# A decoder layer whose projections are FP32 matmuls in 32-column slices in place of three passes over rounded halves

## The chip, the cores and the metric

The kernel runs on one core of one Trainium2 chip (trn2). The metric is the device time of one execution in microseconds, given as the median of the runs. The profile is that of one execution.

## The reference

One pre-norm decoder layer over x of shape 2 x 2048 x 512 and a context of 2 x 154 x 512, all in FP32:

```python
x = x + linear_attention(layernorm(x))          # 16 heads of 32, 128 random features
x = x + cross_attention(layernorm(x), context)  # 16 heads of 32, softmax over 154 keys
x = x + experts(layernorm(x))                   # top 6 of 8 by a softmax router, and a shared one
```

The linear attention projects to q, k and v with `w_qkv` (512 x 1536), takes `elu(q @ proj) + 1` and the same of k as features, sums `k_features^T v` over all keys of a batch, applies it to the queries' features, divides by the sum of features, and multiplies by `w_out`. The cross attention has `x @ W.T + b` for q, k, v and its output, each 512 x 512. The experts are gated units, `silu(h @ gate) * (h @ up) @ down`.

## The kernel before, in words

The 4096 tokens are 8 blocks of 512, four blocks to a batch; a block is four tiles of 128 tokens, and the model dimension of 512 is four chunks of 128. A product of projections is one PSUM bank of 128 x 512, with four chunks to sum over.

Every operand of a product is held as two FP32r tiles (`fp32r` in the profile), the rounded value and what the rounding left. `low` (L116) makes the second: it subtracts the first from the FP32 source. `product` (L144) then makes three matmuls for each chunk, high by high, low by high, high by low, and leaves out low by low. `project` (L151) and `times` (L164) call it for the keys (pk), values (pv), queries (pq) and the cross queries (xpq); `out_tile` (L287) calls it for the two output projections (po_a, po_x), `context_key` and `context_value` for the context's keys (xpk) and values (xpv). The weights are split by `split_weight` (L126), which loads a chunk through the ring of token tiles unless it is loaded already; the layernormed tokens by `transposed` (L240) into the pair xh, xl; the attention by `attended` (at), the cross attention's result by `values` (cx), the context by `context_load`. The experts call `product` too, or have their own loops over the same three terms (L1028, L1141).

The matmuls of linear attention and cross attention that serve single heads are FP32 with 32 columns, into one of four 32-row slices of a bank: the sums over keys (pkv, L397), numerators (pn, L471), denominators (pd, L489) and the context of a head (pc, L720). The scores and features (pp, pqp, psc) use stacked high and low rows of 32 + 32 + 32.

The order of the work is written out by hand as one stream. `Dense` (L175) holds a queue of generators, each a product with its `yield` after every matmul. The stage loops take the features or scores of one step, which the other engines hold up, and before or between them call `dense.fill(n)`, which puts the next n matmuls of the queue; `dense.until` fills until a named tile exists. `dense.after(n, do)` issues a transfer n matmuls later. The stages are:

- L1242: the keys and values of all blocks, with the queries of the first batch from the middle on. Each step is one tile of four key heads: fill, features, and the sums over keys three steps later. Keys and queries go to DRAM and come back stacked by heads (`to_heads`, `stack`, `read`).
- L1285: the second batch's queries; between them the first output projection.
- L1325: cross attention; between its scores the second output projection, the next block's layernorm and the next block's cross queries.
- L1421: the experts.

A scheduler then moves instructions within each engine's stream by a model of their times. All loads of projections' operands go through the queue of SyncE (SP).

Of the kernel before, what the change touches and what calls it, by code (L numbers as in the profile page):

```python
# [19 lines left out]
NC = D // P  # chunks of the model dimension  # L20
# [3 lines left out]
TB = 512  # tokens in a block  # L24
NT = TB // P  # token tiles in a block
# [7 lines left out]
SC = 4  # banks for what is read as soon as it is made  # L33
GROUP = 2  # blocks that a load of an expert serves
# [3 lines left out]
def decoder_layer(  # L38
    ctx: ExitStack,
    tc: tile.TileContext,  # L40
    x: bass.AP,  # [tokens, D]
    ctx_t: bass.AP,  # [D, batch * keys]
    w_qkv: bass.AP,  # [D, 3D]
    proj: bass.AP,  # [HD, H * FEAT]
    w_out: bass.AP,
    b_out: bass.AP,  # [1, D]
    wq_t: bass.AP,  # [in, out], as the three below
# [3 lines left out]
    bq: bass.AP,  # [P, NC]  # L51
    bk: bass.AP,  # [P, NC]
    bv: bass.AP,  # [1, D]
    bo: bass.AP,  # [1, D]
# [13 lines left out]
    bpb = nblk // batches  # blocks of a batch  # L68
# [47 lines left out]
    def low(dst, src, hi, eng=None):  # L116
        """dst = what rounding src to hi left."""
        (eng or nc.vector).tensor_tensor(dst, src, hi.bitcast(F32), ALU.subtract)  # L118

    def load_weight(w, name):  # L120
        raw = eight([P, NC, w.shape[1]], F32, f"raw_{name}")
        for k in range(NC):
            nc.sync.dma_start(out=raw[:, k], in_=w[k * P : (k + 1) * P, :])
        return [raw[:, k] for k in range(NC)]

    def split_weight(raw, name, busy=False):  # L126
        """A weight [D, D] or its loaded chunks as a pair of FP32r parts that sum to it."""
        hi = eight([P, NC, D], FR, f"{name}_hi")
        lo = eight([P, NC, D], FR, f"{name}_lo")
        for k in range(NC):  # L130
            if isinstance(raw, list):
                part = raw[k]
            else:
                part = load_tile(raw, 0, k, name)
            if busy:
                nc.gpsimd.tensor_scalar(hi[:, k], part, 1.0, None, ALU.mult)
            else:
                nc.scalar.copy(hi[:, k], part)
            low(lo[:, k], part, hi[:, k], nc.gpsimd if busy or k % 2 else nc.vector)
        return hi, lo  # L140

    TERMS = ((0, 0), (1, 0), (0, 1))  # all but low times low

    def product(dst, pairs):  # L144
        """dst = sum of a^T b over the pairs (a, b), each of them a (high, low) pair."""
        todo = [(a[i], b[j]) for a, b in pairs for i, j in TERMS]
        for n, (a, b) in enumerate(todo):
            nc.tensor.matmul(dst, lhsT=a, rhs=b, start=n == 0, stop=n == len(todo) - 1)  # L148
            yield

    def project(dst, w, col, src):  # L151
        """dst [P, n] = 128 columns of w, transposed, times src [P, NC, n]."""
        return product(
            dst,
            [
                (
                    (w[0][:, k, col : col + P], w[1][:, k, col : col + P]),
                    (src[0][:, k, :], src[1][:, k, :]),
                )
                for k in range(NC)  # L160
            ],
        )

    def times(dst, src, t, w):  # L164
        """dst [P tokens, n] = the transposed src's tile t, times w."""
        rows = slice(t * P, (t + 1) * P)
        return product(
            dst,
            [
                ((src[0][:, k, rows], src[1][:, k, rows]), (w[0][:, k, :], w[1][:, k, :]))  # L170
                for k in range(w[0].shape[1])
            ],
        )

    class Dense:  # L175
        """Work for the tensor engine that is put, product by product, between the steps of what
        the other engines hold up."""
# [35 lines left out]
        def until(self, made, key):  # L213
            """Fill until made has the key."""
# [8 lines left out]
    def normalize(xs, name, xn=None, pinned=False):  # L223
        """The layernorm of a token tile, in place unless there is an xn."""
# [15 lines left out]
    def transposed(xn, xt, t, name):  # L240
        """A token tile, transposed, into the pair xt of [P, NC, TB]."""
# [25 lines left out]
    def new_xt(name):  # L267
        return [eight([P, NC, TB], FR, f"{n}_{name}") for n in ("xh", "xl")]

# [5 lines left out]
    # A chunk's 4 heads as [high, low, high] of HD rows each, against [high, high, low] on the  # L275
    # other side: one pass over 3 * HD rows is the whole product.
# [10 lines left out]
    def out_tile(name, src, dst, row, parts, w):  # L287
        """dst = src + row + parts (a list over chunks of pairs of [P, tokens]), transposed back,
        times w."""
# [4 lines left out]
        yield from product(po, [(part, (w[0][:, c, :], w[1][:, c, :])) for c, part in enumerate(parts)])  # L294
# [16 lines left out]
    raw = wk  # L311
    wk = [eight([P, NC, D], FR, f"wk_{i}") for i in ("hi", "lo")]
    for t in range(NT):
        pt = ps.tile([P, NC, P], F32, tag="ps", name=f"pt_a0_{t}")
        for c in range(NC):
            nc.tensor.transpose(pt[:, c, :], xs[t][:, c * P : (c + 1) * P], ident)
        hi, lo = (h[:, :, t * P : (t + 1) * P] for h in xts[0])
        a = nc.scalar.copy(hi, pt)
        b = nc.vector.tensor_tensor(lo, pt, hi.bitcast(F32), ALU.subtract)
        c = nc.scalar.copy(wk[0][:, t], raw[t])  # L320
        d = (nc.gpsimd if t % 2 else nc.vector).tensor_tensor(wk[1][:, t], raw[t], wk[0][:, t].bitcast(F32), ALU.subtract)
# [3 lines left out]
    wv = split_weight(wv, "wv")  # L325
# [4 lines left out]
    wq = split_weight(load_weight(w_qkv[:, :D], "wq"), "wq")  # L330
# [10 lines left out]
    def features(src, name, e=None):  # L341
        """src + 1 where src > 0, else exp(src)."""
# [6 lines left out]
    def key_chunk(b, c):  # L349
# [9 lines left out]
        dense.after(8, read)  # L359
# [103 lines left out]
    def numerators(b, c):  # L463
# [36 lines left out]
    def reciprocals(b, pd):  # L500
        """1 / (the denominators of all heads + Z_EPS), spread over the rows of a head."""
# [16 lines left out]
        dense.after(10, turned)  # L518
        dense.after(18 if b < nblk - 1 else 24, stored)
# [16 lines left out]
    def attended(b, c):  # L536
        """The chunk of the block's attention, as a pair."""
        if c == 0:
            ats[b] = [eight([P, NC, TB], FR, f"at{b}_{i}") for i in range(2)]
        at = nums[b][:, c]  # L540
        nc.gpsimd.tensor_tensor(at, at, zrs.pop((b, c)), ALU.mult)
        nc.scalar.copy(ats[b][0][:, c], at)
        low(ats[b][1][:, c], at, ats[b][0][:, c])

    def attention_out(b, t):
# [3 lines left out]
        hi, lo = ats[b]  # L549
        parts = [(hi[:, c, rows], lo[:, c, rows]) for c in range(NC)]  # L550
        yield from out_tile(f"a{b}_{t}", tile_of(x, b, t), tile_of(x1[b], 0, t), bout, parts, wout)

# [20 lines left out]
    def context_load():  # L573
        craw = eight([P, NC, nkeys], F32, "craw")
        nc.sync.dma_start(out=craw, in_=chunked(ctx_t))
        for i in range(2):
            ct.append(eight([P, NC, nkeys], FR, f"ct{i}"))
        nc.scalar.copy(ct[0], craw)
        low(ct[1], craw, ct[0], nc.gpsimd)

    def context_key(c, w):
        pk = bank(f"xpk{c}")[:, :nkeys]
        yield from project(pk, w, c * P, ct)
# [7 lines left out]
    def context_value(bt, first, w, row):  # L591
# [3 lines left out]
        yield from product(  # L595
            pv[:n, :],
            [
                (
                    (ct[0][:, k, at : at + n], ct[1][:, k, at : at + n]),
                    (w[0][:, k, :], w[1][:, k, :]),  # L600
                )
                for k in range(NC)
            ],
        )
# [29 lines left out]
    qts, xsts, es, atts, cxs = {}, {}, {}, {}, {}  # L634

    def cross_query(b, c):
# [3 lines left out]
        yield from project(pq, xwq, c * P, qts[b])  # L640
# [45 lines left out]
    def turn(b, c, t):  # L686
        """The tile's softmax, transposed."""
# [21 lines left out]
    def values(b, c):  # L709
        """The context of the chunk's 4 heads, transposed."""  # L710
        if c == 0:
            cxs[b] = [eight([P, NC, TB], FR, f"cx{b}_{i}") for i in range(2)]
# [16 lines left out]
        nc.scalar.copy(cxs[b][0][:, c], pc)  # L729
        low(cxs[b][1][:, c], pc, cxs[b][0][:, c])  # L730

    def cross_out(b, t):
        if b < 0:
            return
        hi, lo = cxs[b]
        rows = slice(t * P, (t + 1) * P)
        parts = [(hi[:, c, rows], lo[:, c, rows]) for c in range(NC)]
# [814 lines left out]
```

## Time and profile before

| | |
|---|---|
| runs, median (lowest to highest) | 2378.93 us (2378.63 to 2380.4), 3 runs |
| span of the profiled execution | 2379.7 us |
| instructions in it | 35130 |
| TensorE matmuls in it | 11978, of which pk, pv, pq, po_a, xpq and po_x 384 each |
| first features of queries (pqp) | at 240.5 us |
| first scores of the cross attention (psc) | at 685.5 us |
| first product of the experts (pg) | at 1080.9 us |
| mean granted TensorE clock | 0.990 |

The span runs from the first to the last instruction of the program; the profiled execution's own time is this span, and it lies inside the range of the three runs. A row such as `L148 PE MATMUL xpq<-...` gives line, engine, operation, output and inputs; `128*32 128x512` is rows by columns of the stationary operand and the shape of the moving one. PEld is the loading of stationary operands, which overlaps PE. In a row of the time order the first number is the start, the second the time that it and the merged ones after it cover. In the table of stretches each engine's busy time stands in the order PE, PEld, DVE (VectorE), ACT (ScalarE), POOL (GpSimd), followed by the granted clock, the share of the DMA engines' time and GB/s.

### The profile page before, as it was taken

To read this page: it belongs to the slowest core of one execution; us is meant where nothing else is said; L and a number is where in the kernel's file an instruction comes from. 1 tells how busy PE (TensorE), PEld (TensorE's weight loads), DVE (VectorE), ACT (ScalarE), POOL (GpSimd) and SP (SyncE) were. 2 spreads that over 40 slices of the span, in tenths; PEclk is the share of its full clock that TensorE was granted. 3 is DMA by queue.
4 is the path that set the end of the run, shared out by engine and by line. 5 is a ranking of instruction groups with operands and counts; after the bars stand their busy time and mean duration, and the time that the engine had idled before them with its cause. 6 is when DMAs were issued, how large, how long until landed. Compare 5 with 4: busy or idle time off the path is not lost.

```text
span 2379.7 us, 35130 instructions
## 1 busy us (share of the span) xinstructions
PE 2304.3 (97%) x11978; PEld 1739.1 (73%) x11978; DVE 1673.4 (70%) x2777; ACT 1107.8 (47%) x2598; POOL 1217.5 (51%) x1086
## 2 busy tenths in 40 slices
PE   7999999999999999998999989999999999999999
PEld 5777666655556776775778777888778888778887
DVE  7544554456767776777877787677887778977677
ACT  4555666655546776776433333322333223432221
POOL 5444333364537565554655553554565455754543
PEclk9999999999999999998999999999999999999999
DMA  6555767698876556663766655565547555575653
GB/s 210 175 171 166 195 188 190 189 288 227 232 209 188 169 172 176 173 201 135 274 248 224 230 190 213 203 229 212 219 169 274 203 203 217 208 257 193 228 186 128
DMA packets 194896, 485.63 MB, mean 204 GB/s; under 512 B 26970, under 2 KB 46810, under 8 KB 174782
## 3 DMA queue, kind: packets, MB, share of 16 engines
q1 hardware_dynamic: 192990, 477.30, 60.8%
q0 software_dynamic: 1728, 6.09, 0.9%
q8 instruction: 95, 1.56, 0.3%
q14 instruction: 83, 0.68, 0.1%
HBM read 345.01 MB, written 138.31 MB: 203 GB/s over the span
## 4 chain that ended last, share of the span: by engine, by line
PE 73%; DVE 10%; DMA 7%; POOL 4%; issue 3%; ACT 2%; SPq 1%; DVEq 0%; ACTq 0%; POOLq 0%
PE pg L1028 24%; PE pf L1141 10%; PE pq L148 4%; PE pk L148 4%; PE pv L148 3%; PE po_a L148 3%; PE po_x L148 3%; PE pf L148 3%; PE xpq L148 3%; PE pd L489 2%; PE pkv L397 2%; PE pp L382 2%; PE pc L720 2%; PE pqp L457 2%; PE pn L471 2%
## 5 line engine op out<-in xcount | busy, mean ns | idle before, releaser
L1028 PE MATMUL pg<-xo,wq 128*128 128x512 f32 x3360 | 827.0, 393 | 7.2 <-ACT s L1039 3.4
L1028 PEld LDWEIGHTS pg<-xo,wq 128*128 128x128 f32 x3360 | 630.8, 189 | 149.9 <-ACT s L1039 7.2
L1162 DVE TENSOR_TENSOR sum<-sum,pf 128x512 f32<-128x512 f32 x376 | 250.6, 683 | 61.0 <-PE pf L1141 53.5
L387 POOL TENSOR_TENSOR kacc<-kacc,e_k 128x512 f32<-128x512 f32 x128 | 165.5, 1294 | 242.0 <-DVE e_k L346 220.0
L678 ACT ACTIVATE xe<-psc,nb 128x154 f32<-128x154 f32 x512 | 194.3, 404 | 69.5 <-DVE nb L675 56.2
L683 POOL TENSOR_TENSOR xe<-xe,sm 128x616 f32<-128x616 f32 x128 | 157.3, 1237 | 98.9 <-DVE sm L682 64.3
L1091 POOL TENSOR_TENSOR u<-u,gr 128x512 f32<-128x512 f32 x48 | 63.8, 1329 | 255.4 <-DVE u L1060 245.8
L1141 PE MATMUL pf<-ht,wdo 128*128 128x512 f32 x696 | 187.4, 393 | 1.1 <-DVE sum L1162 1.1
L346 DVE SCALAR_TENSOR_TENSOR e_k<-pp,e_k 128x512 f32<-128x512 f32 x128 | 87.4, 686 | 142.2 <-ACT e_k L345 132.4
L1141 PE MATMUL pf<-hb,wdo 128*128 128x512 f32 x522 | 148.2, 399 | 5.9 <-DVE sum L1162 5.8
L1141 PEld LDWEIGHTS pf<-ht,wdo 128*128 128x128 f32 x696 | 129.8, 188 | 30.7 <-DVE sum L1162 1.7
L1059 ACT ACTIVATE u<-u 128x512 f32<-128x512 f32 x80 | 50.6, 632 | 212.2 <-DVE u L1048 209.4
L148 PE MATMUL pf<-wd,hp 128*128 128x512 f32 x528 | 134.0, 400 | 6.0 <-DVE hp L118 2.7
L675 DVE TENSOR_REDUCE nb<-psc 128x2 f32<-128x308 f32 x256 | 111.7, 466 | 24.3 <-PE psc L668 23.7
L148 PEld LDWEIGHTS pf<-wd,hp 128*128 128x128 f32 x528 | 99.7, 190 | 32.9 <-DVE hp L118 3.7
L1141 PEld LDWEIGHTS pf<-hb,wdo 128*128 128x128 f32 x522 | 97.4, 189 | 30.3 <-DVE sum L1162 7.6
L344 ACT ACTIVATE e_k<-pp 128x512 f32<-128x512 f32 x128 | 76.5, 598 | 88.4 <-PE pp L382 85.4
L1048 DVE TENSOR_TENSOR u<-u,pg 128x512 f32<-128x512 f32 x160 | 107.8, 680 | 10.8 <-PE pg L1028 10.0
L678 ACT ACTIVATION_READ_ACCUMULATOR xe<-psc,nb 128x1 f32 x512 | 112.3, 219 | 0.0
L382 PEld LDWEIGHTS pp<-pst,kst 96*128 96x128 f32 x512 | 75.1, 190 | 29.0 <-issue 12.0
L668 PEld LDWEIGHTS psc<-xkst,xst 96*128 96x128 f32 x512 | 76.6, 193 | 25.3 <-issue 9.2
L668 PE MATMUL psc<-xkst,xst 96*128 96x154 f32 x512 | 90.4, 285 | 4.4 <-ACT xe L678 2.8
(280 smaller groups left out, 5185.7 us busy)
## 6 DMA issues: line engine op xcount, KB each, us to landing
wq<-wqs SPq DMA_DIRECT2D x90, 1024.0 KB
wqs<-wq SPq DMA_DIRECT2D x30, 1024.0 KB
wdo<-wds SPq DMA_DIRECT2D x29, 1024.0 KB
kst<-kd SPq DMA_DIRECT2D x96, 256.0 KB
qst<-qd SPq DMA_DIRECT2D x96, 256.0 KB
xst<-xqd SPq DMA_DIRECT2D x96, 256.0 KB
wdo<-wds SPq DMA_DIRECT2D x29, 768.0 KB
kd<-khl SPq DMA_DIRECT2D x32, 512.0 KB
```

The source lines that it names most:

```text
L148: nc.tensor.matmul(dst, lhsT=a, rhs=b, start=n == 0, stop=n == len(todo) - 1)
L346: nc.vector.scalar_tensor_tensor(e, src, 0.0, e, ALU.max, ALU.add)
L382: nc.tensor.matmul(pp[:, h], lhsT=stks[b, c][:, h, rows], rhs=pst[:, head], start=True, stop=True)
L387: nc.gpsimd.tensor_tensor(acc, acc, kp, ALU.add)
L668: nc.tensor.matmul(psc[:, i], lhsT=xsts[b, c][:, h, t * P : (t + 1) * P], rhs=ksts[bt, c][:, h, :], start=True, stop=True,)
L675: nc.vector.tensor_reduce(nb[:, two], psc, AX.X, ALU.max, negate=True)
L678: nc.scalar.activation(e[:, h, :], psc[:, i], AF.Exp, bias=nb[:, h : h + 1], accum_out=sm[:, h : h + 1],)
L683: nc.gpsimd.tensor_tensor(e, e, sm.unsqueeze(2).to_broadcast([P, 4, keys]), ALU.mult)
L1028: nc.tensor.matmul(pb, lhsT=w[:, p, i, k, :], rhs=xop[:, q, k, :], start=first and m == 0, stop=m == len(todo) - 1, skip_group_check=True,)
L1048: nc.vector.tensor_tensor(dst, dst, pb, ALU.add)
L1141: nc.tensor.matmul(banks[i], lhsT=w[:, p, i * P : (i + 1) * P], rhs=t[q], start=new and m == 0, stop=m == len(TERMS) - 1, skip_group_check ...
L1162: nc.vector.tensor_tensor(dst, dst, banks[i], ALU.add)
```

## The change

Weights, layernormed tokens, attention and context are kept as plain FP32 tiles. A product is made by `exact`: for each chunk, the 128 columns of the stationary operand are cut into slices of 32 (64 for the cross query), one FP32 matmul for each slice, each into its own rows of the bank. A unit of the queue is one chunk. The fill counts and timers are set to about a third. The features' and scores' operands are still stored as high and low, and the experts are as they were.

```diff
+COLS = 32
     def load_weight(w, name):
         raw = eight([P, NC, w.shape[1]], F32, f"raw_{name}")
         for k in range(NC):
             nc.sync.dma_start(out=raw[:, k], in_=w[k * P : (k + 1) * P, :])
-        return [raw[:, k] for k in range(NC)]
-    def split_weight(raw, name, busy=False):
...
+        return raw
+    def exact(dst, pairs, width=COLS):
+        for n, (a, b) in enumerate(pairs):
+            m = a.shape[-1]
+            for at in range(0, m, width):
+                cols = slice(at, min(m, at + width))
+                nc.tensor.matmul(
+                    dst[cols, :],
+                    lhsT=a[:, cols],
+                    rhs=b,
+                    start=n == 0,
+                    stop=n == len(pairs) - 1,
+                    skip_group_check=True,
+                )
+            yield
-    def project(dst, w, col, src):
...
+    def project(dst, w, col, src, width=COLS):
+        return exact(dst, [(w[:, k, col : col + P], src[:, k, :]) for k in range(NC)], width)
     def times(dst, src, t, w):
         rows = slice(t * P, (t + 1) * P)
...
+        return exact(dst, [(src[:, k, rows], w[:, k, :]) for k in range(NC)])
@@ transposed
-        nc.scalar.copy(xt[0][:, :, rows], pt)
-        low(xt[1][:, :, rows], pt, xt[0][:, :, rows])
+        nc.scalar.copy(xt[:, :, rows], pt)
@@ out_tile
-        yield from product(po, [(part, (w[0][:, c, :], w[1][:, c, :])) for c, part in enumerate(parts)])
+        yield from exact(po, [(part, w[:, c, :]) for c, part in enumerate(parts)])
@@ the first block: no split of wk, wv, wq
-wk = [eight([P, NC, D], FR, f"wk_{i}") for i in ("hi", "lo")]
...
+        transposed(xs[t], xts[0], t, f"a0_{t}")
@@ key_chunk, numerators, reciprocals, cross_query
-        dense.after(8, read)
+        dense.after(4, read)
-            dense.after(8, lambda: nc.sync.dma_start(out=numd[b][:, c], in_=num))
+            dense.after(4, lambda: nc.sync.dma_start(out=numd[b][:, c], in_=num))
-        dense.after(10, turned)
-        dense.after(18 if b < nblk - 1 else 24, stored)
+        dense.after(5, turned)
+        dense.after(9, stored)
-        dense.after(18, read)
+        dense.after(9, read)
@@ attended
-            ats[b] = [eight([P, NC, TB], FR, f"at{b}_{i}") for i in range(2)]
+            ats[b] = nums[b]
         nc.gpsimd.tensor_tensor(at, at, zrs.pop((b, c)), ALU.mult)
-        nc.scalar.copy(ats[b][0][:, c], at)
-        low(ats[b][1][:, c], at, ats[b][0][:, c])
@@ context_load
-        nc.scalar.copy(ct[0], craw)
-        low(ct[1], craw, ct[0], nc.gpsimd)
+        ct.append(craw)
@@ cross_query
-        yield from project(pq, xwq, c * P, qts[b])
+        yield from project(pq, xwq, c * P, qts[b], 2 * COLS)
@@ values
-        nc.scalar.copy(cxs[b][0][:, c], pc)
-        low(cxs[b][1][:, c], pc, cxs[b][0][:, c])
+        nc.scalar.copy(cxs[b][:, c], pc)
@@ the stage loops (split_weight becomes load_weight for all eight weights)
-        dense.fill(58 if n == 0 else fl(n, 9.25) if n < 32 else fl(n, 9.5))
+        dense.fill(20 if n == 0 else fl(n, 3.1) if n < 32 else fl(n, 3.2))
-        dense.fill(5)
+        dense.fill(2)
-            dense.fill(fl(2 * n + i, 13 if n < 12 else 14))
+            dense.fill(fl(2 * n + i, 4.4 if n < 12 else 4.7))
-            dense.fill(fl(k, 9.5 if b == 0 else 7.75 if b < nblk - 1 else 5.5))
+            dense.fill(fl(k, 3.5 if b == 0 else 2.7 if b < nblk - 1 else 3.0))
```

More of the change, by code (lines that the diff above doesn't have):

```diff
@@ L123, in load_weight @@
             nc.sync.dma_start(out=raw[:, k], in_=w[k * P : (k + 1) * P, :])
-        return [raw[:, k] for k in range(NC)]
-    def split_weight(raw, name, busy=False):
[L128 to L140, printed above, removed]
+        return raw
[13 more added lines that the diff above has]
+            yield
     TERMS = ((0, 0), (1, 0), (0, 1))
@@ L149, in product @@
             yield
-    def project(dst, w, col, src):
[L153 to L162, printed above, removed]
+    def project(dst, w, col, src, width=COLS):
+        return exact(dst, [(w[:, k, col : col + P], src[:, k, :]) for k in range(NC)], width)
     def times(dst, src, t, w):
         rows = slice(t * P, (t + 1) * P)
[L167 to L173, printed above, removed]
+        return exact(dst, [(src[:, k, rows], w[:, k, :]) for k in range(NC)])
     class Dense:
@@ L267, in new_xt @@
     def new_xt(name):
-        return [eight([P, NC, TB], FR, f"{n}_{name}") for n in ("xh", "xl")]
+        return eight([P, NC, TB], F32, f"xt_{name}")
     def load_tile(d, b, t, name):
@@ L310, in decoder_layer @@
     wv = load_weight(w_qkv[:, 2 * D :], "wv")
-    raw = wk
-    wk = [eight([P, NC, D], FR, f"wk_{i}") for i in ("hi", "lo")]
     for t in range(NT):
[L314 to L321, printed above, removed]
+        transposed(xs[t], xts[0], t, f"a0_{t}")
     praw = eight([3 * HD, H * FEAT], F32, "praw")
@@ L324, in decoder_layer @@
         nc.sync.dma_start(out=praw[r * HD : (r + 1) * HD], in_=proj)
-    wv = split_weight(wv, "wv")
     pst = eight([3 * HD, H * FEAT], FR, "pst")
@@ L329, in decoder_layer @@
     low(pst[rest], praw[rest], pst[rest])
-    wq = split_weight(load_weight(w_qkv[:, :D], "wq"), "wq")
+    wq = load_weight(w_qkv[:, :D], "wq")
     kvs, kszs, pkvs, kaccs = [], [], [], []
@@ L548, in attention_out @@
         rows = slice(t * P, (t + 1) * P)
-        hi, lo = ats[b]
-        parts = [(hi[:, c, rows], lo[:, c, rows]) for c in range(NC)]
+        parts = [ats[b][:, c, rows] for c in range(NC)]
         yield from out_tile(f"a{b}_{t}", tile_of(x, b, t), tile_of(x1[b], 0, t), bout, parts, wout)
@@ L575, in context_load @@
         nc.sync.dma_start(out=craw, in_=chunked(ctx_t))
-        for i in range(2):
-            ct.append(eight([P, NC, nkeys], FR, f"ct{i}"))
-        nc.scalar.copy(ct[0], craw)
-        low(ct[1], craw, ct[0], nc.gpsimd)
+        ct.append(craw)
     def context_key(c, w):
         pk = bank(f"xpk{c}")[:, :nkeys]
-        yield from project(pk, w, c * P, ct)
+        yield from project(pk, w, c * P, ct[0])
         kf = half(f"kf{c}")[:, :nkeys]
@@ L594, in context_value @@
         pv = bank(f"xpv{bt}_{first}")
[L595 to L604, printed above, removed]
+        yield from exact(pv, [(ct[0][:, k, at : at + n], w[:, k, :]) for k in range(NC)])
         v = half(f"v{bt}_{first}")
@@ L711, in values @@
         if c == 0:
-            cxs[b] = [eight([P, NC, TB], FR, f"cx{b}_{i}") for i in range(2)]
+            cxs[b] = eight([P, NC, TB], F32, f"cx{b}")
         att, rest, _ = atts.pop((b, c))
@@ L734, in cross_out @@
             return
-        hi, lo = cxs[b]
         rows = slice(t * P, (t + 1) * P)
-        parts = [(hi[:, c, rows], lo[:, c, rows]) for c in range(NC)]
+        parts = [cxs[b][:, c, rows] for c in range(NC)]
         yield from out_tile(f"x{b}_{t}", tile_of(x1[b], 0, t), tile_of(x2[b], 0, t), bor, parts, xwo)
@@ L1247, in decoder_layer @@
         if (b, c, t) == (nblk - 1, 1, 0):
-            xwk = split_weight(wk_t, "xwk")
+            xwk = load_weight(wk_t, "xwk")
             dense.add(*(context_key(i, xwk) for i in range(NC)))
         if (b, c, t) == (nblk - 1, 2, 0):
-            xwv = split_weight(wv_t, "xwv")
+            xwv = load_weight(wv_t, "xwv")
             bvr = half("bvr")
@@ L1278, in decoder_layer @@
     res = attending.enter_context(tc.tile_pool(name="res", bufs=1))
-    wout = split_weight(w_out, "wout")
+    wout = load_weight(w_out, "wout")
     steps = chunks[bpb * NC :]
@@ L1316, in decoder_layer @@
         if n == 10:
-            xwq = split_weight(wq_t, "xwq")
+            xwq = load_weight(wq_t, "xwq")
         if n == 11:
@@ L1339, in decoder_layer @@
                     bor = load_row(bo, "bor")
-                    xwo = split_weight(wo_t, "xwo")
+                    xwo = load_weight(wo_t, "xwo")
             if b == 0 and k == 0:
```

## The prediction

> **What bounds the kernel now.** I read the page's busy shares first, then its slices, then a table of stretches, and only then single instructions in order of time.
>
> ```profile
> PE 2304.3 (97%) x11978; PEld 1739.1 (73%) x11978; DVE 1673.4 (70%) x2777; ACT 1107.8 (47%) x2598; POOL 1217.5 (51%) x1086
> ...
> PEclk9999999999999999998999999999999999999999
> ```
>
> TensorE is busy 97% of the span at its full clock; no other engine passes 70%. A share can hide stages, so the stretches follow: keys and values (0 to 240 us), keys with queries (to 480), queries with output products (to 685), cross attention (to 1081), and the way into the experts.
>
> ```profile
> 0.00:240.00 240.00, 225.35 (x1497) 176.50 (x1497) 129.12 (x203) 126.29 (x218) 120.72 (x135) 0.99 0.60 179
> 240.00:480.00 240.00, 238.94 (x1517) 157.58 (x1516) 125.37 (x202) 157.72 (x289) 86.00 (x76) 1.00 0.70 194
> 480.00:685.00 205.00, 200.23 (x916) 107.04 (x912) 127.60 (x202) 107.38 (x198) 96.50 (x90) 0.98 0.90 254
> 685.00:1081.00 396.00, 376.97 (x2437) 285.07 (x2435) 294.60 (x683) 276.67 (x1133) 235.28 (x242) 0.99 0.61 176
> 1081.00:1180.00 99.00, 91.50 (x437) 67.52 (x437) 81.57 (x132) 48.24 (x115) 47.19 (x42) 0.93 0.58 207
> ```
>
> The first pair of numbers behind the length is TensorE: idle 14.7, 1.1, 4.8, 19.0 and 7.5 us, 47 us of 1180. Every stage that has projections is held by TensorE. So the question is what one projection costs it before and after, and the answer must come from start-to-start distances: a matmul's own duration contains its pipeline latency.
>
> ```profile
> 270.38 0.39 PE L148 MATMUL pq<-xl_a,wq_hi 128*128 128x512 f32 x1
> 270.61 0.39 PE L148 MATMUL pq<-xh_a,wq_hi 128*128 128x512 f32 x1
> 270.84 0.39 PE L148 MATMUL pq<-xh_a,wq_lo 128*128 128x512 f32 x1
> 271.16 0.62 PE L489 MATMUL pd<-e_q,ksz 128*32 128x512 f32 x1
> 271.16 0.63 PE L489 MATMUL pd<-eq,ksz 128*32 128x512 f32 x3
> 271.61 0.59 PE L489 MATMUL pd<-e_q,ksz 128*32 128x512 f32 x1
> 271.62 0.60 PE L489 MATMUL pd<-eq,ksz 128*32 128x512 f32 x3
> 272.15 0.50 PE L148 MATMUL pq<-xl_a,wq_hi 128*128 128x512 f32 x1
> 272.49 0.39 PE L148 MATMUL pq<-xh_a,wq_hi 128*128 128x512 f32 x1
> 272.72 0.39 PE L148 MATMUL pq<-xh_a,wq_lo 128*128 128x512 f32 x1
> ```
>
> These ten rows hold both forms. pq is a projection as it is now: one full-width pass each 0.23 us (eleven distances of a run of twelve xpq matmuls, from 722.15 to 724.64 us, give 0.2264). pd (L489) is what the change makes of it: FP32, 128 rows by 32 columns by 512, four heads in four column slices. The program has four such matmuls here, the trace eight: each FP32 matmul is two instructions. Four start together, the other four 0.45 us later, and the next product 0.53 us after those. The same is seen where rounds follow each other: pc's, inside its sixteen instructions at 719 us, stand 0.4295 us apart in the raw starts (719.428, 719.857, 720.287).
>
> **The change part by part.** *A product.* A projection of 128x512 has four chunks of the model dimension. Before: 4 x 3 passes x 0.2264 = 2.72 us. After: 4 chunks x 2 halves = 8 rounds of four slices x 0.4295 = 3.44 us. That is 0.72 us more. There are 6 kinds (keys, values, queries, first output, cross query, second output) x 8 blocks x 4 = 192 of them: **+138 us**. The context's products: four of 308 columns (pitch now 0.141 us, 12 passes, 1.69 us; a round estimated at 0.26 us, between 0.43 for 512 columns and 0.114 for pkv's 128, so 2.1 us) and four of values (12 x 0.23 = 2.76 against 3.44 us): **+4 us**.
>
> Two rules bear on this step. The Trainium skill, "FP8 and Floating Point Precision", TensorE Precision Notes, says that true FP32 takes four passes through the array (high and low of one side by high and low of the other): it speaks against the change, since the kernel now makes three. At the 0.2264 us of a pass here it would give 4 x 4 x 0.2264 = 3.62 us a product, +174 us in all; the row's rounds are 0.4295 / 2 = 0.215 us a pass and give +138. I take the row. "TensorEngine Tiling (Array Packing)", Theoretical Speedup, promises up to four times from 32-column tiles. The row agrees that four slices take the time of one (pd alone with one head at a time, 273.28 us, has two halves in 1.04 us where four heads take 1.06). But this is against narrow matmuls one after another; a 128-column projection already fills the array. Read as four times over today's 2.72 us it would give 192 x -2.04 = -392 us; the row excludes it.
>
> *The 64-column cross query* (32 of the 192) has no row. Bounds: its two slices run side by side as four do (3.44 us, nothing on top), or one after the other (16 x 0.43 = 6.87 us, +110 us). I take the first: pd's and pc's slices are the same kind of thing.
>
> *Changes of array width.* Read in the rows above: 270.84 to 271.16 is 0.32 (+0.09), the first round 0.45 (+0.02), out of it 0.53 (+0.10), the first full pass after 0.34 (+0.11): 0.32 us for going in and out. In the order of the two built programs TensorE changes width 556 times before and 714 after, so 79 pairs more, nearly all in cross attention, where projections stand between full-width scores and transposes: **+25 us**. In the key stages the number stays, since pkv was already narrow.
>
> *Broken rounds.* The same order has 68 groups more than whole rounds of the FP32 512-column slices need, 41 before: the scheduler lets a score or another projection in between. 27 x 0.86 = 23 us at most; some pair up with a neighbour's free slices. Value taken **+18 us**, bounds 5 and 23.
>
> *What is removed elsewhere.* Roundings and differences: on VectorE at 28.9, cx 21.8, xl_x 21.3, xl_a 21.8 us and the weights', on ScalarE at 19.6 us and the weights' casts. None is on TensorE, so this pays only out of TensorE's 47 us of idle time. Of that, 7.8 us before the first transpose stays, and transfers (qst 4.5, kst 3.0, xst 1.4) meet a slower consumer and mostly vanish. wk_lo's 2.9 us, the 1.9 us at khl, xl_x's 3.6 and at's 1.1 go with their instructions; the first pk then waits for the cast of the transposes and gains some 2 us. VectorE's att and sm waits shrink, since VectorE has less to do in a longer stage. I take **-20 us**; bounds 0 and -39 (all but the first 7.8).
>
> *Moved.* The fill counts and timers are about a third, as the units are three times longer; a read of a stored chunk (kst, 4 units of 0.86 us instead of 8 of 0.23) is issued on SP's queue some 1.6 us later, and what stands behind it on SP moves by as much. The cover is a queue of projections ready ahead of the features (20 units, 17 us); if it is gone, TensorE waits those 1.6 us a chunk, 32 times, 51 us at worst, and I count it with the third rival. Weight loads keep their sizes and count (five weights, four transfers of 256 KB each); they no longer pass through the five-deep ring of token tiles. A unit of work put before a score is now 0.86 us instead of 0.23, so the scores (ScalarE waits for them) stand behind longer pieces; ScalarE has 30% free there. Experts (after 1180 us) are the same instructions: 0.
>
> *Sum.* 138 + 4 + 25 + 18 - 20 = 165 us on the profiled span of 2379.7 us: 2544.7. The runs' median is 2378.9, 0.8 us less: **2544 us**.
>
> **The rivals.** (1) *The two 64-wide slices do not overlap*: +110 us, about 2654. Against it: nothing in the rows separates two slices from four. (2) *TensorE is no longer filled*: the coarse units and the later reads leave holes. For it: the last block of cross attention has 7.5 us idle in 99 already, and its fill falls from 5.5 to 3 units. With no idle time paid back and 40 us of new waits: 2604. (3) *Everything is paid back*: all idle time but the start goes, broken rounds cost 5 and half of the width changes fall into waits: 2380 + 138 + 4 + 12 + 5 - 39 = 2500. (4) *On the other side, faster*: the four slices share one moving operand, while in each narrow row of the trace (pn, pd, pc, pkv) each slice has its own. If sharing lets the array read it once per half, a round falls to one pass, 0.216 us: 1536 rounds x -0.2135 = -328, so 2217 us. It would decide from a round of 0.4295 - 165 / 1536 = 0.32 us. Against it: four slices with four operands run no slower than one with one, so reading is not what sets the 0.43.
>
> **How the numbers follow.** The main case 79%, its own range 2515 to 2580 (paid-back waits 0 to 39, broken rounds 5 to 23, width changes half to all). Rival 1: 6%; rival 2: 6%; rival 3: 6%; rival 4: 3%. The range 2495 to 2605 takes in the main case and rivals 2 and 3 and leaves out 1 and 4 and the far ends. Faster by over 0.2% (about what a measurement of this kernel tells from no change) only in rival 4: 3%; within 0.2% needs a round of just that price: 1%; slower: 96%.
>
> **What would show it.** Right: eight rounds of projection slices 0.43 us apart, a product of keys in 3.4 to 3.5 us; the first pqp near 270, the first psc near 760 to 770, the first expert product (pg) near 1240 us; TensorE idle for under 35 us before the experts, VectorE's share down, the experts' stretch still 1200 us. Wrong: rounds of another pitch; xpq's starts 0.43 us apart one by one (rival 1); idle time over 60 us in cross attention (rival 2); a projection that takes less than 2.7 us (rival 4).

## The result and the profile after

| | before | after |
|---|---|---|
| runs, median (lowest to highest) | 2379.66 us (2378.63 to 2381.91), 4 runs | 2573.89 us (2569.15 to 2577.2), 4 runs |
| after / before | | 1.0809 (95% interval 1.0791 to 1.0827) |
| span of the profiled execution | 2379.7 us | 2567.4 us |
| first pqp / first psc / first pg at | 240.5 / 685.5 / 1080.9 us | 274.4 / 799.6 / 1268.4 us |
| TensorE idle in the three stages up to these marks | 14.6, 5.8, 19.0: 39.5 us | 19.4, 36.4, 8.1: 64.0 us |
| from the first pg to the end | 1298.8 us | 1299.0 us |

The change makes the kernel 8.1% slower. The forecast was 2544 us with a range of 2495 to 2605: the sign and the range held, and the value was 30 us too low. In the profile 34 us come in the first stage, 80 in the second, 73 in the cross attention and none in the experts.

The page of the changed kernel, its busy shares and the slices' granted clock, answering to the two rows of before:

```profile
PE 2468.4 (96%) x15418; PEld 1502.9 (59%) x15418; DVE 1577.2 (61%) x2633; ACT 1071.9 (42%) x2533; POOL 1179.9 (46%) x1069
...
PEclk9999999999899999999999999999999999999999
```

TensorE has 164 us more of work, VectorE 96 us less: the removed roundings are gone, and in the kernel before TensorE had waited only some 8 us for them (xl_x 3.9, wk_lo 2.9, at 1.1, cx 0.6). The same kernel cut at its three marks (TensorE first behind the length, granted clock third from the end):

```profile
0.00:274.40 274.40, 254.98 (x2508) 106.88 (x2508) 105.30 (x174) 116.88 (x203) 106.68 (x127) 0.99 0.54 158
274.40:799.60 525.20, 488.77 (x3949) 182.02 (x3948) 222.82 (x362) 243.75 (x452) 167.92 (x162) 0.97 0.68 188
799.60:1268.40 468.80, 460.66 (x3218) 208.23 (x3216) 260.55 (x611) 269.67 (x1111) 226.81 (x236) 1.00 0.52 149
1268.40:2567.40 1299.00, 1263.98 (x5747) 1005.78 (x5747) 988.51 (x1488) 441.62 (x770) 678.49 (x546) 0.99 0.57 211
```

The second row is the surprise: with projections a quarter dearer, TensorE should wait less, yet it is idle for 36.4 us there, and its clock is 0.97 on average. The list of TensorE's waits (total, times, longest, over the whole span) names what it waits for:

```profile
PE pp L358 <- DMA kst<-kd: 15.1, 17, 2.4
PE pqp L433 <- DVE e_q L322: 9.9, 2, 5.2
PE pn L447 <- DVE xr_a L281: 8.7, 1, 8.7
...
PE pqp L433 <- DMA qst<-qd: 5.3, 2, 3.9
```

The wait for keys coming back from DRAM (kst) was 3.0 us before and is 15.1 now, 4.0 of it in the second stage. How the next two arise is seen on TensorE and on VectorE at 681 to 694 us:

```profile
680.92 1.04 PE L465 MATMUL pd<-e_q,ksz 128*32 128x512 f32 x8
686.66 0.80 PE L433 MATMUL pqp<-qst,pst 96*128 96x512 f32 x1 [4.69 <-DVE e_q L322]
692.64 0.80 PE L433 MATMUL pqp<-qst,pst 96*128 96x512 f32 x1 [5.18 <-DVE e_q L322]
693.36 5.82 PE L134 MATMUL po_a<-raw_wout,num 128*32 128x512 f32 x32
```

```profile
685.12 0.69 DVE L217 BATCH_NORM_STATS2 st_x<-xsx 128x6 f32<-128x512 f32 x1 [14.74 <-DMA xsx<-x]
...
690.84 0.69 DVE L217 BATCH_NORM_STATS2 st_x<-xsx 128x6 f32<-128x512 f32 x1 [4.24 <-DMA xsx<-x]
```

VectorE, in order, stands for 14.7 us before a token tile that was only just written (x) and read back (xsx); the features e_q stand behind it, and TensorE behind those. The last TensorE row shows a second price: 32 instructions of one product take 5.82 us where elsewhere they take 3.64. In the raw starts the rounds at 694.218, 695.071 and 695.925 are 0.853 us apart, then 0.43 again. The same stretch by the granted clock, and one at 144 us:

```profile
144.00:146.00 2.00, 2.00 (x15) 0.93 (x18) 0.02 (x1) 1.65 (x4) 0.00 (x0) 0.71 0.00 0
146.00:148.00 2.00, 2.00 (x12) 0.22 (x4) 1.27 (x2) 0.47 (x1) 1.25 (x1) 0.50 0.00 0
```

```profile
688.00:692.00 4.00, 0.00 (x0) 0.00 (x0) 1.16 (x3) 0.09 (x1) 0.00 (x0) 0.50 0.96 216
692.00:696.00 4.00, 3.36 (x17) 0.96 (x21) 3.29 (x8) 1.63 (x3) 2.69 (x3) 0.50 0.70 169
696.00:700.00 4.00, 4.00 (x33) 0.91 (x25) 1.74 (x4) 0.00 (x0) 3.79 (x6) 0.77 0.43 131
```

In both places TensorE waited and then ran at half its clock, with work to do: from 144.86 to 148.27 us, and from 692.64 to 697.82 us. So a wait can cost more than its length. The Trainium skill, "TensorE: Matmul & The Clock Gate", Part 1, says this of idle windows of about 3.4 us, with a window that runs freely. The rows agree on the half, and with 3.4 and 5.2 us of work roughly on the time to recover; but ahead of the stretch at 144 stood a wait of only 1.60 us (before 143.62 us), while one of 1.59 us before 186.96 us had no such stretch behind it. I count this loss, for every profile below, as TensorE's busy time in each 2 us times one less the granted clock.

### The profile page after: what moved, and what is told of

The parts are those of the page before. It is cut to its first block, busy times and chain, and to the rows that moved or that the text cites. A ratio compares the mean times of both kernels' runs of the same rounds, so it can differ in the third digit from the quotient of the medians.

```text
span 2567.4 us, 41736 instructions
## 1 busy us (share of the span) xinstructions
PE 2468.4 (96%) x15418; PEld 1502.9 (59%) x15418; DVE 1577.2 (61%) x2633; ACT 1071.9 (42%) x2533; POOL 1179.9 (46%) x1069
## 4 chain that ended last, share of the span: by engine, by line
PE 39%; DVE 4%; POOL 3%; DMA 2%; issue 2%; ACT 1%; SPq 0%; DVEq 0%; ACTq 0%; POOLq 0%
PE pg L987 24%; PE pf L1100 10%; PE pf L150 3%; PE po_x L134 1%; DMA wq<-wqs 1%; POOL sum L1124 1%; DMA rgu<-in_w_up 1%; POOL hp L119 1%; DVE u L1007 0%; DVE wq L119 0%; DVE sum L1121 0%; DVE xo L119 0%; PE pto L1139 0%; DVE u L1019 0%; DMA wds<-wdq 0%
## 5 line engine op out<-in xcount | busy, mean ns | idle before, releaser
L1121 DVE TENSOR_TENSOR sum<-sum,pf 128x512 f32<-128x512 f32 x376 | 251.2, 683 | 56.8 <-PE pf L1100 49.2
L134 PE MATMUL pq<-xt_a,raw_wq 128*32 128x512 f32 x1024 | 137.9, 594 | 0.0
L134 PE MATMUL pk<-xt_a,raw_wk 128*32 128x512 f32 x1024 | 131.5, 601 | 0.7 <-ACT xt_a L233 0.7
L134 PE MATMUL po_x<-raw_xwo,cx 128*32 128x512 f32 x1024 | 131.8, 604 | 0.0
L134 PE MATMUL po_a<-raw_wout,num 128*32 128x512 f32 x1024 | 129.7, 613 | 0.0
L134 PE MATMUL xpq<-xt_x,raw_xwq 128*64 128x512 f32 x512 | 127.1, 604 | 0.0
L134 PE MATMUL pv<-raw_wv,xt_a 128*32 128x512 f32 x1024 | 123.1, 593 | 0.0
L358 PEld LDWEIGHTS pp<-pst,kst 96*128 96x128 f32 x512 | 66.9, 191 | 92.6 <-issue 69.6
```

Of the source, the lines that this page charges most:

```text
L134: nc.tensor.matmul(dst[cols, :], lhsT=a[:, cols], rhs=b, start=n == 0, stop=n == len(pairs) - 1, skip_group_check=True,)
L358: nc.tensor.matmul(pp[:, h], lhsT=stks[b, c][:, h, rows], rhs=pst[:, head], start=True, stop=True)
L1121: nc.vector.tensor_tensor(dst, dst, banks[i], ALU.add)
```

## The experiments

Two readings of the result were open at first. **Theory A**: the four passes cost what was forecast, and the extra comes from the fill counts, which were cut to a third where the work of the queue was not (below). **Rivals**: the slices themselves are dear (a cut product costs more than a whole one), or the 64-column cross query is. In the end both the counts and the cut came out as causes.

A ledger for all profiles comes first, since each verdict uses it. "Before pg" is the span up to the experts' first product, which is where everything happens. Broken groups are those beyond whole rounds of the FP32 512-column slices, and width changes those of TensorE's columns, both counted in the built program's order, as in the prediction. (Incomplete groups can be counted in other ways, which give up to 6 more or fewer; the prices fitted below then move by at most 4 us, 0.02 us and 0.03 us.)

| kernel | ratio to before (95%) | before pg, us | idle | lost to the clock | broken groups | width changes |
|---|---|---|---|---|---|---|
| before | 1 | 1080.9 | 39.5 | 8.0 | 41 | 556 |
| after | 1.0809 (1.0791 to 1.0827) | 1268.4 | 64.0 | 10.9 | 68 | 714 |
| f1 whole | 1.0683 (1.0665 to 1.0700) | 1236.9 | 32.7 | 11.4 | 92 | 542 |
| f2 cross query in 32 | 1.0909 (1.0879 to 1.0939) | 1293.4 | 69.5 | 25.1 | 79 | 696 |
| h1 cross query whole | 1.0764 (1.0734 to 1.0794) | 1259.6 | 64.5 | 18.2 | 63 | 602 |
| h2 cross query and outputs whole | 1.0667 (1.0630 to 1.0705) | 1232.3 | 52.5 | 12.1 | 70 | 512 |
| f4 counts raised | 1.0704 (1.0680 to 1.0727) | 1246.5 | 45.6 | 10.6 | 56 | 800 |
| g1 whole, counts raised | 1.0527 (1.0507 to 1.0546) | 1201.9 | 29.1 | 5.8 | 58 | 546 |
| g3 whole, counts of before | 1.0520 (1.0502 to 1.0539) | 1200.6 | 21.5 | 3.3 | 58 | 570 |
| g4 cut, counts of before | 1.0741 (1.0725 to 1.0757) | 1258.5 | 38.4 | 8.9 | 76 | 862 |
| f6 only outputs changed | 1.0189 (1.0170 to 1.0209) | 1130.7 | 44.8 | 8.2 | 40 | 636 |
| g2 one pass in place of three | 0.9379 (0.9356 to 0.9401) | 929.4 | 115.7 | 79.4 | 94 | 552 |
| i1 layernorm later | 1.0834 (1.0812 to 1.0855) | 1282.4 | 67.3 | 21.9 | 68 | 714 |
| i2 counts raised, layernorm later | 1.0720 (1.0690 to 1.0749) | 1255.3 | 49.2 | 15.6 | 56 | 800 |

**f1: no cutting.** One FP32 matmul of all 128 columns for each chunk, all else as after.

```diff
-COLS = 32
+COLS = 128
```

> The changed kernel with the slices left whole: one FP32 matmul of 128 columns for each chunk, also for the cross query. Theory (four passes a chunk, whatever the width): a pass at the pitch of a full-width one, 4 x 4 x 0.2264 = 3.62 us a product against 3.44 cut in four and 3.84 cut in two (as the trace of after shows xpq), so 160 x 0.18 - 32 x 0.22 = +22 us; the programs' orders have 86 in-and-out pairs of width changes fewer (-27 us) and some 20 us of broken rounds of numerators and denominators more. Together +15 us on 2574: 2565 to 2605. Rival (the cut is what makes FP32 affordable, since weight loads of 128 FP32 columns, 0.19 us each, are no longer covered or slices share the array): each of 8 instructions a product costs 0.19 us or more on top, +290 us and up, over 2800.

Measured: 2545.6 us. The time of one product in order of time, first in the changed kernel, then whole:

```profile
306.31 3.64 PE L134 MATMUL pk<-xt_a,raw_wk 128*32 128x512 f32 x32
```

```profile
406.63 3.70 PE L134 MATMUL pk<-xt_a,raw_wk 128*128 128x512 f32 x8
```

32 instructions and 8 instructions take the same time: eight steps of 0.43 us. In the raw starts a round of four slices is 0.429 us (61.721, 62.150, 62.579) and a whole half 0.430 us (60.165, 60.595). I had expected 0.453 for the whole half, twice the pass of before, and so a time at or above that of the cut form; that was wrong, and the rival of over 2800 us as well. Cutting an array-filling product into slices buys nothing here, and the changed kernel pays the switching for it. Part of f1's gain lies elsewhere: its idle time is 32.7 us in place of 64.0, and though it has the same fill counts it waits only 0.5 us for kst.

**f2 and h1: the cross query in 32-column slices, and whole.** In f2 `2 * COLS` becomes `COLS` in `cross_query`, in h1 it becomes `P`.

> The changed kernel with the cross query cut in slices of 32, not 64. Theory: a round of two 64-wide slices takes 0.48 us in the trace of after, one of four 32-wide ones 0.43, so 32 products x 8 x 0.05 = -13 us, less some 5 us for a few more broken rounds: 2559 to 2570. Rival (a round costs the same at any width, and the 0.48 is made of waits for operands): no change, 2570 to 2577, and xpq's starts stay 0.48 us apart.

> The changed kernel with the cross query alone as whole FP32 matmuls of 128 columns. Theory (a half of a whole matmul costs what a round of two or four slices costs, 0.43 us; slices cost only by width changes and by what breaks their rounds): 56 in-and-out pairs of width changes fewer, -18 us, 5 broken rounds fewer, -4: 2552 on 2574, or 2545 to 2560, all of it in the cross attention. Rival (width changes are free where the matmul after them waits anyway): 2565 to 2577.

Measured: f2 2599.9 us, h1 2566.6 us. Both expectations missed, and h1's time lies in its rival's range (2565 to 2577). For f2 I had read a round of 64-column slices as 0.48 us; most of these rounds are 0.42 to 0.43 us apart, so there was nothing to gain, and 26 us were lost. The ledger puts the profile's 25.0 us to the clock (14.2 us more lost than in after), 11 more broken groups (8 us at the price found below) and 5.5 us of idle time. For h1 the ledger tells why it was little: 112 width changes fewer, but 0.5 us more idle and 7.3 us more lost to the clock. Net of idle time, clock and five broken groups at the 0.74 us found below, h1 gives -8.8 - 0.5 - 7.3 + 3.7 = -12.9 us for 56 pairs of changes: **0.23 us a pair**, not 0.32. Against the rival, the width changes are therefore not free; that the clock loss belongs to h1's change isn't shown.

**h2: cross query and outputs whole**, only keys, values and queries cut; as h1, and `out_tile` calls `exact(..., P)`.

> The changed kernel with slices of 32 for keys, values, first queries and the context alone; both outputs and the cross query are whole. Theory: 101 pairs of width changes fewer than the changed kernel, -32 us, broken rounds +2: 2543 on 2574, or 2535 to 2552, with kst's waits and VectorE's late layernorm as before, since the key stage's order and counts stay. Rival (the cut's cost sits in the key stage, where it delays keys): 2560 or more.

Measured: 2540.9 us, as expected. The waits for kst stay at 13.5 us, so the cutting of the outputs isn't what makes them. But VectorE's late layernorm, which I had expected to stay, did not. The second stage of h1, where the outputs are still cut, and of h2:

```profile
277.30:803.60 526.30, 491.30 (x3922) 184.83 (x3921) 224.18 (x364) 244.01 (x452) 169.44 (x163) 0.97 0.68 188
273.70:789.40 515.70, 505.00 (x3329) 196.04 (x3328) 217.15 (x353) 244.46 (x451) 165.51 (x158) 0.99 0.69 189
```

TensorE is idle there for 35.0 us in h1 and 10.7 in h2; the waits for e_q and xr_a are gone from it in h2, and VectorE's longest wait for a token tile (xsx) falls from 14.7 to 7.6 us. Half of this comes back in the cross attention (22.9 us idle in place of 10.9). So the waits at 681 to 694 us belong to the cut output products. Over all runs the same line divides them: with cut outputs VectorE's longest wait for xsx is 12.2 us or more, with any counts; with whole outputs it is 8.8 or less. Why a cut product of the same length makes the tile late isn't shown.

**f4: the two fill counts of the key stage raised.** A block of this stage puts 16 units each of keys, values and queries into the queue, and 4 transposes of two units each: 56. The stage takes 16 steps of 3.1, some 50 units. In the kernel before it was 152 units against 16 x 9.25 = 148. The transposes kept their two units while all else went to a third.

```diff
-        dense.fill(20 if n == 0 else fl(n, 3.1) if n < 32 else fl(n, 3.2))
+        dense.fill(20 if n == 0 else fl(n, 3.5) if n < 32 else fl(n, 3.6))
```

> The changed kernel with the fill counts of the key stage raised from 3.1 and 3.2 to 3.5 and 3.6 units a step. Theory (the counts are a third of the old ones, but the two units of each transpose were not cut to a third, so a block has 56 units for 50 that are filled; the queue falls behind, keys are forced just before they are needed, and what is left over shifts the output products and the layernorm onto late transfers): waits for kst fall from 15 us to under 6, those of pqp and pn behind VectorE (20 us) fall by half or more, while 43 pairs of width changes more cost up to 14 us; net -5 to -20 us, 2553 to 2570. Rival (the waits come from the later reads and SP's queue, not from the counts): kst's waits stay at 12 us or more and the time at 2570 to 2590.

Measured: 2548.8 us, 25 us faster than after. The idle time falls from 64.0 to 45.6 us, and the waits for kst to 0.9. The other half of the theory missed: pqp and pn still wait 18.3 us for VectorE (21.0 in after), and e_q and xr_a now lead the waits:

```profile
PE pn L447 <- DVE xr_a L281: 8.2, 1, 8.2
PE pqp L433 <- DVE e_q L322: 7.7, 3, 4.5
```

How far the keys are ahead can be read from the starts: from the end of a chunk's last pk to its first use by pp there are, in the mean of the 32 chunks, 16.6 us in before, 12.3 in after, 25.1 in f4, but also only 14.4 in f1, which hardly waits. So the low counts do thin the cover, and in the whole form what is left still suffices. Of the 25 us some 9 are twelve broken groups fewer, at the price found below, and not waits.

**g1, g3, g4: counts and cutting apart.** g1 is f1 with the raised counts. g3 and g4 yield three times after each chunk and take all counts and timers of the kernel before, whole (g3) and cut (g4).

> The changed kernel with whole FP32 matmuls of 128 columns and the key stage's fill counts raised to 3.5 and 3.6. Theory (a whole half costs what a round of four slices does, 0.430 us, and what remains over the four passes is broken rounds of the numerators and denominators, of which this order has 117 against 150 in the uncut one): 33 x 0.86 = -28 us on 2546, less some for changed waits: 2515 to 2532. Rival (the counts paid in the cut form because keys came late; the uncut form has only 10 us of idle time before the cross attention, so nothing is left to gain): 2540 to 2550.

> Whole FP32 matmuls of 128 columns with the old kernel's fill counts and timers, a chunk's unit yielding three times as three passes did. Theory (four passes and nothing else): 2380 + 192 x (8 x 0.430 - 2.72) = +138, context +4, 11 broken rounds more +9, 7 pairs of width changes +2: 2533, or 2515 to 2535 with idle time paid back; TensorE idle no more than before. Rival (the FP32 form loses time wherever it is put, through coarser units): 2545 or more, with more idle time.

> The changed kernel (slices of 32, cross query 64) with the old fill counts and timers and three yields for a chunk. Theory (passes, width changes and broken rounds make the time, the counts little): 138 + 4, 35 broken rounds more than before +30, 156 pairs of width changes more, the most of all, +50: 2380 + 222 = 2602, or 2580 to 2605 with idle time paid back. Rival (the new counts cost the changed kernel most of what it lost beyond the passes): under 2560.

Measured: g1 2507.0, g3 2503.9, g4 2556.3 us, all below what was expected; g4's is in its rival's range. g3's stages up to the experts:

```profile
0.00:270.00 270.00, 260.99 (x1290) 137.22 (x1290) 110.15 (x177) 121.66 (x207) 108.13 (x129) 1.00 0.54 162
270.00:777.30 507.30, 504.66 (x2110) 209.23 (x2106) 218.67 (x360) 245.28 (x447) 165.75 (x161) 1.00 0.69 193
777.30:1200.50 423.20, 413.34 (x2187) 239.23 (x2186) 255.17 (x614) 269.39 (x1119) 223.21 (x233) 0.99 0.55 164
```

Here TensorE's idle time does what I had forecast for the change: 21.5 us in place of 39.5, and 3.3 lost to the clock in place of 8.0, which is -22.7 us against the forecast's -20. So in differences of the table's ratios (per cent of the kernel before): four passes for three cost 5.2% (124 us), the cutting 2.2% with these counts (g4 against g3, 53 us) and 1.3% with the new ones (after against f1, 30 us), and the new counts 0.7% in the cut form (after against g4, 16 us) and 1.6% in the whole (f1 against g3, 39 us). So g4's rival had the number, but not the reason: the counts are 16 us of the 70 or so that after loses beyond the passes. None of these kernels beats the kernel before.

Idle time and clock loss together, against before, put the four side by side:

| us | counts of before | new counts |
|---|---|---|
| whole | -22.7 (g3) | -3.4 (f1) |
| cut in slices | -0.2 (g4) | +27.4 (after) |

The new counts add 19 us in the whole form and 28 in the cut one, the cut 23 with the old counts and 31 with the new. Each cell is one profile, and two profiles of the same work can differ by 5 to 7 us (last section).

**f6: only the outputs changed**, with the counts of before: the kernel before with FP32 slices for po_a and po_x and three yields a chunk.

> The kernel before with the two output projections alone (64 of the 192 products) as FP32 in slices of 32; a chunk's unit yields three times, so all fill counts and timers stay as they were. Theory (price of rounds and of width changes, no waits): 64 x 0.72 = +46 us, 40 pairs of width changes more, +13 us: 2380 + 59 = 2439, or 2425 to 2445 with some idle time paid back. Rival (most of the loss is waits that the new counts make): only rounds' price or less, under 2420, or with the price of a third of the loss by share of products, 2379 + 65 = 2444, but then with over 20 us more idle time of TensorE than before.

Measured: 2429.4 us, in the forecast's range, and the rival's 20 us of idle time are not there: 44.8 us in place of 39.5. But the idle time has moved. The second stage, where before was idle for 5.8 us:

```profile
239.50:709.40 469.90, 445.95 (x2907) 234.49 (x2904) 235.74 (x383) 250.01 (x460) 180.48 (x169) 0.98 0.76 210
```

It is 24.0 us there, as in g4 (24.0), with 13.1 us of waits for e_q, and 10.8 us less in the cross attention.

**g2: the other direction.** The kernel before with one pass (high by high) in place of three; the two products with the rounded-off parts are left out.

> The kernel before with one pass for each chunk of a projection in place of three: high by high alone, so it leaves out both products with a rounded-off part; those parts are still made, and a chunk's unit yields three times, so counts and timers stay. Theory (every stage with projections is held by TensorE, so passes are worth their pitch until the next engine holds): 192 x 8 x 0.2264 = -348 us at most; VectorE and ScalarE were busy 382 and 391 us of the 685 before the cross attention and 295 and 277 of its 396, which leaves about -290 us: 2050 to 2120. Rival (TensorE only looks full and the stages wait for others): less than half of the passes' price comes back, over 2205.

Measured: 2231.6 us, so the rival was right and my theory wrong: two passes of 0.2264 us fewer in 768 chunks are -348 us, and 147 came. TensorE's waits:

```profile
PE pqp L464 <- DMA qst<-qd: 17.5, 6, 6.0
PE psc L675 <- ACT xe L685: 9.1, 19, 1.5
...
PE pt_x L251 <- DVE xr_x L302: 7.7, 3, 4.1
PE pp L389 <- DMA kst<-kd: 7.3, 6, 2.5
```

The ledger says where the rest went: 76 us more of idle time, spread over transfers and engines, **71 us more lost to the halved clock**, and 53 broken groups (39 us at the price found below): -348 + 76 + 71 + 39 = -162, against -152 in the profile. TensorE is the bound at three passes by a small margin only, and with one pass the waits were paid nearly twice.

**i1, i2: the late token tile.** The layernorm of the cross attention's first block enters the queue one chunk later, in after (i1) and in f4 (i2). TensorE's order keeps its counts; VectorE's and SP's change around 685 us.

```diff
-        if n == 7:
+        if n == 8:
             ln, tr = layernorm(x1[0], 0, 0, qts, "x")
...
-        if n == 8:
+        if n == 9:
             dense.add(*tr[:1], *ln, *tr[1:])
```

> The changed kernel with the layernorm of the cross attention's first block put into the queue one chunk later, after another block's output products instead of right behind the ones that it reads. TensorE's order of instructions, its broken rounds (68) and width changes (714) stay as in the changed kernel; only VectorE's and SP's order moves, around 685 us. Theory: VectorE standing in order before a token tile that is not yet back from DRAM (14.7 us at 685, then 4.2) makes the features e_q late, TensorE waits 9.9 us for them there and runs at half its clock for about 9 us after it (about 4.5 us lost): idle of the second stage 36.4 to about 26, the granted clock of 1.00 around 690 us, and 10 to 16 us in all: 2557 to 2564. It would fall at 2569 and above (the wait is only moved to the next late tile), or if the clock stays at a half there without the wait.

> The same move in the changed kernel with the raised counts (3.5 and 3.6, which alone gave 2548.8). TensorE's order stays as in that one (56 broken groups, 800 width changes). It still had 7.7 us of TensorE waiting for e_q and 8.5 us lost to the halved clock in the second stage. Theory: 8 to 14 us less, 2535 to 2541, the second stage's idle 28 to about 20. Rival (the wait behind xr_a at the end of the stage, 8.2 us, is the one that ends last, and takes over what is saved): 2545 to 2550.

Measured: 2582.7 and 2556.6 us. The theory fell, and i2 lies above its rival's range too. i1's head of the waits:

```profile
PE pp L358 <- DMA kst<-kd: 16.8, 16, 2.3
PE po_a L134 <- DVE xr_a L281: 10.3, 1, 10.3
PE pqp L433 <- DMA qst<-qd: 10.1, 3, 5.2
```

The wait for e_q is gone, and one of 10.3 us for xr_a and 4.8 us more of qst stand in its place: it moved. That i1 is slower than after isn't shown: its interval overlaps that of after, and 6.7 us of its profile's 14 stand in the first stage, ahead of the edit, where it lost 6.6 us to the clock and after 1.7. Which transfer, if any, has to come earlier to take these 10 us out of the cut form stays open; whole outputs take them out (h2).

**What the ledger fits.** Over the ten changed kernels from after to f6 in the table (g2 left out), before-pg time less idle time and clock losses is fitted by three prices, to within about 6 us for each (f6, with a third of the products, counts a third of the first): **123 us for the change of passes** in all products (0.64 us a product), **0.20 us for a pair of width changes** and **0.74 us for a broken group**. The two last runs come out at 159.7 and 157.0 us where it gives 158.1 and 157.7; as TensorE's counts in them are those of after and f4, this shows that the ledger repeats, and is no new test of the prices. These prices are a fit, not single measurements.

## Why the prediction came out as it did

For the changed kernel the fit gives 123 + 79 x 0.20 + 27 x 0.74 = 159 us of work and, with 24.5 us of idle time and 2.9 us of clock loss, 186 us; the profile has 187.5 up to the experts.

- **The bound, right.** TensorE sets every stage with projections, and the added passes were not hidden anywhere: 34, 80 and 73 us in the three stages, and the experts within 0.2 us.
- **The product's price, right in kind, somewhat high.** Eight rounds 0.43 us apart stand in the trace as forecast. By the fit the change of passes costs 123 us where +138 and +4 were forecast. The forecast compared an undisturbed run of twelve passes (2.72 us a product) with undisturbed rounds. In place, the passes of before take 2.98 us a product from each start to the next TensorE instruction's (572 us over 192), waits among them, so the old form was dearer than its best row. How much of the 19 us that explains isn't settled.
- **Width changes and broken rounds, right in count.** +25 came to 16 by the fit, since a pair costs 0.20 us in the mean; the one place I had read (0.32 us) was not typical. +18 came to 20.
- **The step that failed: "I take -20 us" for the idle time that TensorE would win back.** It came out as +24.5 us and 2.9 us of clock, 47 us on the wrong side. The reason behind it (the removed work and a slower consumer let waits vanish) holds for whole products with the old counts: g3 has -22.7. It failed in two places. First, the prediction passed over the counts as "about a third, as the units are three times longer" and didn't add up what a block puts in (56 units) against what the steps take (50). It had named the danger, a cover of ready projections that is gone, and priced it at 51 us at worst (under the third rival, where only the second has new waits), but did not ask whether the cover lasts. It also counted the 1.9 us at khl as gone with its instruction, which stays. The queue falls behind, the keys are forced out just before they are needed, and kst is waited for 17 times. Second, the cut form waits more by itself, which the prediction put at nothing: with the old counts (g4) nothing is won back, -0.2 us, and the cut outputs bring VectorE's late token tile. The table above gives each of the two 19 to 31 us. Raising the two counts alone brought the time to 2548.8 us, 5 us from the forecast, with 8.7 us more idle time and clock loss than before in place of 20 less, so that nearness is no confirmation.
- **What hid part of the error.** The products (-19), the widths (-9) and the rounds (+2) come to 26 us less than forecast, against the 47 us of the idle time: 21 of the 23 us by which the profiled execution missed. That errors of other terms made up for more than half of this one was luck. The rest of the 30 us is mostly that this execution's span, 2567.4 us, lies 6.5 us below the runs' median.
- **The rivals.** The 64-column slices do run side by side (f2 gained nothing by 32). Rival 2, holes in TensorE's work at 2604 us, is the nearest to what happened: it had 40 us of new waits, and there were 24.5 net, in the key and query stages and not at the end of the cross attention, where I had looked for them (idle 8.1 us there). Rival 3, waits paid back, is in part what g3's idle time shows, without the cutting. Rival 4, a shared moving operand at half the price, is refuted by rounds of 0.43 us.
- **The marks.** First pqp at 274.4 us (270 was forecast), first psc at 799.6 (760 to 770), first pg at 1268.4 (1240), idle before the experts 64.0 us (under 35). The second mark is the one that named the failed step: it is 30 to 40 us late, and its stage idle for 31 us more than before.

## What to carry to other kernels

Cutting a matmul that fills the array into column slices made nothing faster here: one step of four slices takes as long as one of the whole width, and each change of width among other work is paid on top. When units of a hand-filled queue change their size, add up what each step of the schedule puts in and takes out, small items included: here a queue that fell behind by a tenth thinned the cover of its loads, and together with the cut form turned them into waits of the bounding engine. Don't assume that idle time won back in one form is won back in another. And price TensorE's waits above their length, and changes that speed TensorE up below their full gain: with one pass, 76 us more of idle time came with 71 us more lost to the clock.

## What the runs showed of the hardware

- A whole FP32 matmul of 128 columns by 512 is two steps of 0.430 us (f1); four slices of 32 take 0.43 us a step, two of 64 mostly the same, and in about a quarter of their steps 0.48 (after). The slices of a round start mostly 6 or 7 ns apart at the full clock (after).
- The granted clock was one half behind waits of TensorE, for 3.4 and 5.2 us of work in the two places shown (after); ahead of one of them stood a wait of only 1.60 us, and one of 1.59 us elsewhere had nothing behind it. It weighs in three runs: 71 us of g2 (against before), 14 us of f2 and 7 us of h1 (against after).
- The stretch ahead of an edit varied by 6.7 us between two profiles with the same instructions of TensorE there (i1 and after), 4.9 us of it by the clock.
